# Local attention blocks: normalised keys to the block diagonal by DMA, and the low half of the first feed-forward weights on GpSimd

## The chip, the core and the metric

The kernel runs on one core of a Trainium2 chip. The metric is the device time of one execution in microseconds; the time before is the median of three runs. The engines are named as the profile names them: PE is TensorE (PEld its weight loads), DVE is VectorE, ACT is ScalarE, POOL is GpSimd, and SP is SyncE, which issues the DMAs of this kernel in one queue.

## The reference

The program runs eight layers on an activation of 4 to 8 sequences: a Mamba-like scan, a stack of local attention blocks, token attention, the same stack of local attention blocks again, linear attention, and three closing stages. The change touches only the two passes through the local attention stack. One stack has six levels, each of which is, cut to what matters:

```
for i in range(DEPTH):                       # 6 levels, 16 heads of 64, window 32
    x = attn_layer(shift_tokens(x), Wqkv[i], q_scale[i], k_scale[i], Wo[i]) + x
    x = ffn_layer(shift_tokens(x), ln_g[i], ln_b[i], W1[i], b1[i], W2[i], b2[i]) + x

attn_layer:  q, k = l2norm(q) * qs, l2norm(k) * ksc        # per token and head
             q, k = rotary(q) , rotary(k)
             softmax(mask(q @ [k of window before, k of own window].T * 8)) @ v
ffn_layer:   xn = layernorm(x) * g + bln
             a, gate = split(xn @ W1 + b1)                 # 341 + 341 columns
             a * gelu(gate) @ W2 + b2
```

Everything is float32.

## The kernel before

**Tiling.** The activation is 8 sequences of 256 tokens by 128 features, kept with features on the partitions and cut into NCH = 4 chunks of 512 tokens (two sequences). In the local stack the 16 heads are taken in 8 pairs. A *unit* is one chunk at one level, so a pass has 24 units of 8 pairs, and the loop in `steps` (L607) runs over the pairs of all units one after the other: 192 pairs in a pass, 384 in both, and some lead-in and run-out.

**Software pipeline.** One turn of that loop is a *step*. Each of its calls `do(what, ahead)` works on another pair: `rotate` on the pair 6 ahead, `prep` 1 ahead, `project` 7 ahead, `rounded` 5 ahead, `norms` and `norms_end` 6 ahead, `scores` on the current pair, `share` and `shared` 1 behind, `turn` and `attend` 2 behind. `feed` advances the feed-forward part of an older unit by one of 8 pieces a step. The loop stands under a manual schedule: each engine executes its instructions in the order in which this code writes them, and waits on semaphores for the others.

**Keys, lines 406 to 415.** `project` (L329) multiplies a pair's query and key weights with the chunk (three rounded float32 products, L213 to L215), copies both 128x512 results from PSUM to `raw` (ACT, L338), multiplies them with the cosine table into `tt` (DVE, L340), and has two DMAs swap the upper and lower 64 partitions of `raw` into `sw` (SP, L343 and L344). One step later `rotate` (POOL, L367 and L368) multiplies `sw` with the sine table and adds it to `tt`: `tt[:, 0]` is the rotated query and `tt[:, 1]` the rotated key. The squares go through ACT (L348) and PE (L359); every fourth pair the norms are finished on ACT and DVE (L131 to L146), four small DMAs (L388) bring them to 32 partitions, and ACT and POOL split them into a high and a low part (L397, L398). `prep` spreads the norms over a pair's 128 partitions by one matmul (PE, L410) into a PSUM bank `rb` and writes the normalised key into `kb`:

```
for h in range(2):
    nc.vector.scalar_tensor_tensor(kb[:, h, 32:], tt[:, 1], self.hcol[:, h:h + 1], rb, ALU.mult, ALU.mult)
```

`kb` is block-diagonal: 128 partitions, two column blocks, one for each head of the pair. `hcol[:, h]` holds one on the partitions of head h and zero elsewhere, so each of the two instructions writes a whole 128x512 block, half of it zeros. The 32-partition quarters 0 and 2 belong to head 0, and 1 and 3 to head 1. There are two `kb` buffers, zeroed once. `scores` (PE, L429) multiplies queries with `kb` one step later; DVE scales, masks, reduces and subtracts the scores (L437 to L440), ACT takes the exponential (L450), DVE the sums and reciprocals (L460, L461), POOL divides (L469), PE transposes (L482), ACT copies (L485), and PE multiplies with the values (L505).

**First feed-forward weights, lines 288 to 301.** `load_1` runs as a side generator that advances once a step. For each of the six column groups of `W1` (order 3, 4, 5, 0, 1, 2: the gate half first) it loads the raw weights in one step; in the next PE makes the bias (L296), ACT writes the high part scaled by the layer norm's gain (L298), DVE makes the low part in one instruction (L299), and DVE adds the bias (L301). It is queued at p = 7 of the last chunk's feed; the next unit's feed reads gate groups 3 to 5 at its p = 4 and groups 0 to 2 at its p = 6, one step a pair. `split` (L198) is the helper that other weights use: ACT writes the high part (L202) and POOL subtracts for the low part (L203), which is put into the list `top` and so issued first thing in the next step.

**PSUM.** Most products take their bank from a ring of six (`RING`), so a product waits until the bank's user of six takes ago has been read.

**Queue.** All DMAs here are issued by SP in program order. In the built program each DMA waits for the one that stands eight before it on SP, since eight semaphores are used in turn.

Of the kernel before, what the change touches and what calls it, by code (L numbers as in the profile page):

```python
# [11 lines left out]
F32R = mybir.dt.float32r  # L12
BF = mybir.dt.bfloat16
AF = mybir.ActivationFunctionType
ALU = mybir.AluOpType
# [6 lines left out]
NCH = 4  # L22
# [21 lines left out]
def f32(ap):  # L44
    return ap.bitcast(F32)


class Arena:
# [3 lines left out]
    def __init__(self, big, at=0, end=SIZE, rounded=None):  # L52
        self.big, self.at, self.end, self.tags, self.rounded = big, at, end, {}, rounded
# [164 lines left out]
class LocalBlock:  # L218


    def __init__(self, k):
        self.k, self.nkb = k, 0
        nc = k.nc
        R = Arena(k.bigr, 0, RSIZE)
        self.P = P = Arena(k.big, k.con.at, SIZE, R)
        self.D = k.D
        self.mask = k.const(P, "c_mask", (128, 512), BF)
        self.hcol = k.const(P, "c_hcol", (128, 2))
        self.sel = k.const(P, "c_sel", (128, 2, GP, 32))
        bsel = P.tile([128, GP, 128], F32, name="c_bsel", tag="rr", bufs=1)  # L230
        nc.sync.dma_start(out=bsel, in_=k.a["c_bsel"])
        self.bsel = P.tile([128, GP, 128], F32R, name="bsel")
        nc.vector.tensor_copy(self.bsel, bsel)
        self.qs = k.const(P, "qs", (128, DEPTH, 4))
        self.ffc = k.const(P, "lngb", (128, DEPTH, 2))
        self.b2 = k.const(P, "b2", (128, DEPTH))
        self.b1 = k.const(P, "b1", (128, DEPTH, 6))
        self.zero = P.tile([32, 128], BF, name="zero")
        self.kb = [P.tile([128, 2, 32 + CT], F32, name="kb_%d" % i) for i in range(NKB)]
        self.y = [P.tile([128, 2, 257], F32, name="y_%d" % c) for c in range(NCH)]  # L240
        for t in [self.zero] + self.kb + self.y:
            nc.vector.memset(t, 0.0)

        for tag, n, bufs in (("fx", 512, 2), ("sq", 512, 3), ("lny", 128, 2), ("nwt128", 128, 2),
                             ("tab0", 512, 2), ("tab1", 512, 2), ("wr_64", 512, NWR), ("wr_128", 256, NWR),
                             ("wvo", 512, NWV), ("bias1", 8, 2), ("w2", 128, 3)):
            P.place(tag, n, bufs)
        for tag, n, bufs in (("xs", 1024, 2), ("wqk", 512, 9), ("w1", 256, 7), ("fh", 1024, 1), ("rs", 512, 2)):
            R.place(tag, n, bufs)

        self.rs, self.nrs = [P.tile([128, CT], F32R, name="rs", tag="rs") for _ in range(2)], 0
        for t in self.rs:
            nc.vector.tensor_scalar(t, self.mask, 0.0, None, ALU.mult)
# [34 lines left out]
    def load_1(self, w, l):  # L288
        k, P, nc = self.k, self.P, self.k.nc
        w.bias1 = P.tile([128, 6], F32, name="bias1", tag="bias1", bufs=2)  # L290
        for i in (3, 4, 5, 0, 1, 2):
            m, o = (128, 128, 85)[i % 3], 341 * (i // 3) + 128 * (i % 3)
            r = self.raw(k.a["w1"][l, :, o:o + m], (128, m), "rw1")
            yield
            bp = k.bank(RING)
            nc.tensor.matmul(bp[:m, 0:1], r, self.ffc[:, l, 1:2], start=True, stop=True)  # L296
            hl = P.tile([128, 2, m], F32R, name="w1hl", tag="w1", bufs=7)
            nc.scalar.activation(hl[:, 0], r, AF.Copy, scale=self.ffc[:, l, 0:1])  # L298
            nc.vector.scalar_tensor_tensor(hl[:, 1], r, self.ffc[:, l, 0:1], f32(hl[:, 0]), ALU.mult, ALU.subtract)  # L299
            w.w1[i] = hl  # L300
            nc.vector.tensor_tensor(w.bias1[:m, i:i + 1], bp[:m, 0:1], self.b1[:m, l, i:i + 1], ALU.add)  # L301

    def load_2(self, w, l):
# [102 lines left out]
    def prep(self, u, p):  # L406

        k, nc, tt, rs = self.k, self.k.nc, u.t[p], u.rs[p // GP]
        rb = k.bank(RING)
        nc.tensor.matmul(rb, self.bsel[:, p % GP], rs, start=True, stop=True)  # L410
        kb = self.kb[self.nkb % NKB]
        self.nkb += 1
        for h in range(2):
            nc.vector.scalar_tensor_tensor(kb[:, h, 32:], tt[:, 1], self.hcol[:, h:h + 1], rb, ALU.mult, ALU.mult)  # L414
        u.kb[p] = kb

    def scores(self, u, p):
# [189 lines left out]
    def steps(self, us, ws, depth):  # L607
        NU, done, feed, side = len(us), [0] * NCH, None, []
        for i in range(-LEAD, 8 * NU + 20):
            def do(what, ahead):  # L610
                n, p = (i + ahead) // 8, (i + ahead) % 8
                if 0 <= n < NU:
                    what(us[n], p)
                    return us[n], p
                return None, p
            for f in self.top:
                f()
            self.top.clear()
            do(self.rotate, 6)
            do(self.prep, 1)  # L620
            do(self.share, -1)
            u, p = do(self.project, 7)
            do(self.rounded, 5)
            do(self.shared, -1)

            side = [g for g in side if next(g, side) is not side]
            if u:
                last = u.l + 1 == depth
                if u.c == NCH - 1 and not last:
                    side.append(self.load_qk(ws[u.l + 1], u.l + 1, p))  # L630
                    if p in (4, 5):
                        side.append(self.load_tab(ws[u.l + 1], u.l + 1, p - 4))
            do(self.norms, 6)
            do(self.norms_end, 6)
            n, p = (i - 12) // 8, (i - 12) % 8
            if 0 <= n < NU:
                u = us[n]
                last = u.l + 1 == depth
                if p == 0:
                    feed, fed = self.feed(u), u  # L640
                next(feed)
                if p == 7:
                    done[u.c] += 1
                    if u.c == NCH - 1 and not last:
                        side += [self.load_1(ws[u.l + 1], u.l + 1), self.load_2(ws[u.l + 1], u.l + 1)]
                    if last:
                        self.end(u.c)
            do(self.attended, -3)
            do(self.turn, -2)
            for f in self.mid:  # L650
                f()
            self.mid.clear()
            do(self.scores, 0)
            u, p = do(self.values, 2)
            if u and u.c == NCH - 1 and u.l + 1 < depth and p % 2 == 0:
                side.append(self.load_v(ws[u.l + 1], u.l + 1, p // 2))
            do(self.attend, -2)
            do(self.squares, 7)
            do(self.soft, 0)
            if feed and fed.late:  # L660
                self.k.nc.scalar.preload_act_table_set("natural_log_exp_and_others")
                fed.late = False
            n, p = (i + LEAD) // 8, (i + LEAD) % 8
            if p == 0 and 0 <= n < NU:
                u = us[n]
                assert done[u.c] == u.l
                u.xs = self.k.split(self.P, self.y[u.c][:, :, 0:256], (128, 2, 256), "xs", 2, self.top)
                u.xs = u.xs.rearrange("p h b t -> p h (b t)")
                if n + 1 < NCH:
                    side.append(self.begin(n + 1))  # L670
                    next(side[-1])
        assert not side
# [698 lines left out]
def constants():  # L1371
    f = np.float32
    h = np.arange(0, 64, 2, dtype=f)
# [9 lines left out]
    rot = np.zeros((128, 4, T), f)  # L1383
# [5 lines left out]
    i = np.arange(32)[:, None]  # L1389
    j = np.arange(64)[None]  # L1390
    m = np.zeros((128, 2, 4, 2, 32), f)
# [5 lines left out]
    sel = np.zeros((128, 2, GP, 32), f)  # L1397
    bsel = np.zeros((128, GP, 128), f)
    head = (np.arange(128) // 32) % 2
    for pl in range(GP):  # L1400
        for s_ in range(2):
            for h_ in range(2):
                row = 2 * GP * s_ + 2 * pl + h_
                sel[:, s_, pl, row] = head == h_
                if s_:
                    bsel[row:64:32, pl] = np.where(head == h_, f(-0.5), f(0))
    hcol = (head[:, None] == np.arange(2)[None]).astype(f)
    sm = (np.arange(128)[:, None] // 16 == np.arange(8)[None]).astype(f)
    d16 = np.arange(128) // 16
    dm = (d16[:, None] == d16[None]).astype(f)  # L1410
# [2 lines left out]
    p = np.arange(128)  # L1413
    sely = (2 * np.arange(16)[None, :, None] + p[:, None, None] // 64 == np.arange(32)[None, None]).astype(f)
    i2 = (p[:, None] % 64 == np.arange(64)[None]).astype(f)
    more = {"c_sely": sely, "c_i2": i2, "c_bmask": bm, "c_smask": sm, "c_dmask": dm, "c_hsel": hs}
    return {**more, "c_rot": rot, "c_mask": m.reshape(128, 512).astype("bfloat16"), "c_sel": sel, "c_bsel": bsel, "c_hcol": hcol}


def layout(i):  # L1420
# [55 lines left out]
def build(inputs, stages=None):  # L1476
    d = layout(inputs)
    d.update(constants())
    return {n: np.ascontiguousarray(v) for n, v in d.items()}
# [16 lines left out]
```

## Time and profile before

| what | value |
|---|---|
| median of 3 runs | 4397.36 us (4397.0 to 4401.22) |
| the profiled execution, its own time | 4402.16 us |
| its span, first to last instruction | 4400.4 us |
| first and last norm matmul of the local passes (L410) | 623.3 and 4006.4 us |
| norm matmuls (L410), one for each pair | 384 |
| L414 on DVE | 768 instructions, 537.7 us busy |
| granted PE clock, mean over the span | 0.922 |

The local passes lie between about 640 and 2190 us and between 2440 and 4010 us; what lies ahead, between and behind them is other code and is not touched. Within each pass PE stays at 9 tenths or more of every slice, and the page's clock row shows 9 tenths or more there. How to read the views: the busy share of an engine in a stretch says how full it is; the list of waits says which engine's instruction ended the idle time of another; the chain that ended last follows from the end of the program backwards what released what.

### The profile page before, as it was taken

How to read it: one execution, taken by the hardware profiler on the slowest of the kernel's cores; microseconds unless marked ns; L12 is line 12 of the kernel's file. 1: busy time of each engine (PE TensorE's matmuls, PEld its weight loads, DVE VectorE, ACT ScalarE, POOL GpSimd, SP SyncE). 2: the span in 40 equal slices, each digit the busy share in tenths (PEclk: the TensorE clock that was granted, in tenths of full speed). 3: DMA queues.
4: the chain of work that ended last, by engine and by line, in shares of the span. 5: the costliest groups of instructions: out<-in, count | busy, mean ns of one | idle time of the engine just before them, and what ended most of it. 6: DMA issues, size and time to landing. Idle time of an engine off the chain costs nothing.

```text
span 4400.4 us, 147972 instructions
## 1 busy us (share of the span) xinstructions
PE 3760.2 (85%) x64201; PEld 2852.7 (65%) x64201; DVE 3705.8 (84%) x5687; ACT 2645.0 (60%) x5050; POOL 3078.2 (70%) x1546
## 2 busy tenths in 40 slices
PE   5656679999999999999966899999999999997376
PEld 2222257777778778777744777787787777775144
DVE  6999958888888888888876788888888888887988
ACT  5423347767667677677544676676676767764322
POOL 3656668878778778787575887787877877862433
PEclk7777889999999999999966999999999999998578
DMA  0000033323233233333202332232333323221000
GB/s 19 7 3 16 1 78 81 89 74 89 72 75 90 73 85 74 78 82 76 54 20 68 81 90 72 69 93 72 88 74 74 87 71 92 72 71 42 15 6 10
DMA packets 134900, 272.97 MB, mean 62 GB/s; under 512 B 31020, under 2 KB 68328, under 8 KB 134248
## 3 DMA queue, kind: packets, MB, share of 16 engines
q1 hardware_dynamic: 134248, 263.51, 23.9%
q8 instruction: 503, 8.24, 0.8%
q14 instruction: 149, 1.22, 0.1%
HBM read 49.50 MB, written 6.29 MB: 13 GB/s over the span
## 4 chain that ended last, share of the span: by engine, by line
DVE 38%; PE 37%; ACT 13%; issue 8%; POOL 2%; DMA 2%; SPq 0%; DVEq 0%; POOLq 0%; ACTq 0%
PE pb L505 6%; PE pb L325 5%; DVE big L340 4%; DVE big L816 4%; DVE big L414 4%; PE pb L429 3%; DVE big L460 3%; PE pb L563 3%; PE pb L359 3%; DVE pb L438 2%; DVE big L439 2%; PE pb L410 2%; DVE pb L437 2%; DVE big L440 2%; ACT big L348 2%
## 5 line engine op out<-in xcount | busy, mean ns | idle before, releaser
L367 POOL TENSOR_TENSOR big<-big 128x1024 f32<-128x1024 f32 x384 | 916.0, 2385 | 405.0 <-DMA big<-big 319.7
L368 POOL TENSOR_TENSOR big<-big 128x1024 f32<-128x1024 f32 x384 | 917.2, 2389 | 30.1
L325 PE MATMUL pb<-big 128*32 128x128 f32 x24576 | 748.8, 274 | 4.3 <-DVE big L301 4.0
L414 DVE SCALAR_TENSOR_TENSOR big<-big,pb 128x512 f32<-128x512 f32 x768 | 537.7, 741 | 193.7 <-PE pb L410 153.3
L325 PEld LDWEIGHTS pb<-big 128*32 128x32 f32 x24576 | 681.6, 111 | 12.9 <-DVE big L301 7.1
L327 ACT COPY big<-pb 128x512 f32<-128x512 f32 x768 | 439.1, 597 | 317.8 <-PE pb L325 316.0
L338 ACT COPY big<-pb 128x512 f32<-128x512 f32 x768 | 440.1, 585 | 280.3 <-PE pb L215 248.6
L340 DVE TENSOR_TENSOR big<-pb,big 128x512 f32<-128x512 f32 x768 | 482.6, 668 | 43.6 <-ACT big L338 43.0
L469 POOL TENSOR_TENSOR big<-big 128x1024 f32<-128x1024 f32 x192 | 365.6, 1904 | 217.2 <-ACT big L348 133.6
L348 ACT ACTIVATE big<-big 128x512 f32<-128x512 f32 x768 | 443.4, 629 | 0.0
L505 PE MATMUL pb<-big 128*32 128x128 f32 x11520 | 402.0, 278 | 43.8 <-ACT big L485 35.0
L817 POOL TENSOR_TENSOR big<-big 128x1024 f32<-128x1024 f32 x128 | 305.3, 2398 | 191.4 <-DVE big L816 186.3
L213 PE MATMUL pb<-bigr 128*128 128x512 f32 (+1 forms) x1056 | 429.6, 407 | 11.3 <-ACT bigr L298 8.9
L215 PE MATMUL pb<-bigr 128*128 128x512 f32 (+1 forms) x1056 | 422.0, 400 | 4.2 <-DVE bigr L299 3.7
L429 PE MATMUL pb<-big 128*32 128x128 f32 x12288 | 418.6, 277 | 7.7 <-DVE big L440 4.7
L214 PE MATMUL pb<-bigr 128*128 128x512 f32 (+1 forms) x1056 | 420.1, 398 | 1.0 <-POOL bigr L203 1.0
L505 PEld LDWEIGHTS pb<-big 128*32 128x32 f32 x11520 | 325.3, 111 | 107.2 <-ACT big L485 91.4
L429 PEld LDWEIGHTS pb<-big 128*32 128x32 f32 x12288 | 314.9, 110 | 110.0 <-ACT big L338 32.7
L810 PE MATMUL pb<-bigr 128*128 128x512 f32 x512 | 214.0, 533 | 181.2 <-DVE big L816 124.6
L437 DVE TENSOR_TENSOR pb<-pb,big 128x512 f32<-128x512 f32 x384 | 266.4, 694 | 69.7 <-PE pb L429 67.3
L450 ACT ACTIVATE big<-big 128x1024 f32<-128x1024 f32 x192 | 203.7, 1061 | 191.5 <-DVE big L440 179.1
L359 PE MATMUL pb<-big 128*32 128x128 f32 x6144 | 296.4, 275 | 19.2 <-DVE big L146 8.6
(270 smaller groups left out, 7400.6 us busy)
## 6 DMA issues: line engine op xcount, KB each, us to landing
big<-big SPq DMA_DIRECT2D x768, 256.0 KB, 3.5
big<-in_wqk SPq DMA_DIRECT2D x96, 128.0 KB, 3.4
big<-x SPq DMA_DIRECT2D x28, 256.0 KB, 2.8
big<-in_c_rot SPq DMA_DIRECT2D x24, 256.0 KB, 4.9
big<-in_wv SPq DMA_DIRECT2D x48, 128.0 KB, 3.9
big<-in_wo SPq DMA_DIRECT2D x48, 128.0 KB, 3.3
big<-big SPq DMA_DIRECT2D x384, 16.0 KB, 2.4
x<-big SPq DMA_DIRECT2D x20, 256.0 KB, 3.9
```

Source lines behind the costliest of these rows:

```text
L213: mm(out, w[:, 0], x[:, 0], start=start, stop=False)
L325: nc.tensor.matmul(vp[32 * h:32 * h + 32, bass.ts(w, 128)], xw, wv[:, bass.ts(h, 128)], start=True, stop=True)
L327: nc.scalar.copy(v2[:, 4 * q:4 * q + 4].rearrange("p w f -> p (w f)"), vp)
L338: nc.scalar.copy(raw[:, s], ps)
L340: nc.vector.tensor_tensor(tt[:, s].rearrange("p (b t) -> p b t", b=2), ps.rearrange("p (b t) -> p b t", b=2), ct, ALU.mult)
L348: nc.scalar.activation(sq, raw[:, s], AF.Square)
L359: self.k.nc.tensor.matmul(u.nrm[32 * i:32 * i + 32, 0:128], self.sel[:, j, pl], q[:, bass.ts(i, 128)], start=(pl == 0 and j == 0), stop=(p ...
L367: nc.gpsimd.tensor_tensor(s4, s4, u.w.tab[1][:, :, None, :].broadcast_to([128, 2, 2, T]), ALU.mult)
L368: nc.gpsimd.tensor_tensor(tt, tt, sw, ALU.add)
L414: nc.vector.scalar_tensor_tensor(kb[:, h, 32:], tt[:, 1], self.hcol[:, h:h + 1], rb, ALU.mult, ALU.mult)
L429: mm(s4[32 * w:32 * w + 32, 2 * wg:2 * wg + 2], qf[:, 32 * win:32 * win + 32], kb[:, :, 32 * win:32 * win + 64].rearrange("p h (o j) -> p ...
L505: mm(u.acc[32 * w:32 * w + 32, bass.ts(wg, 128)], pts[o][:, 32 * win:32 * win + 32], v2[:, win - 1 + o], start=False, stop=(g == 3 and o = ...
```

## The change

`prep` multiplies the rotated key with the spread norms in place, with one DVE instruction, and four DMAs on SP copy the four 32-partition quarters to the diagonal blocks of `kb`. The off-diagonal blocks keep the zeros of the start, and the mask column `hcol` with its load is gone. `load_1` scales the raw weights in place on ACT and then uses the helper `split`: ACT writes the high part, POOL the low part in the next step. `load_1` is queued three steps earlier, at p = 4 of the last chunk's feed, behind that step's piece of `feed`; `load_2` stays at p = 7.

```
-        self.hcol = k.const(P, "c_hcol", (128, 2))
...
-            hl = P.tile([128, 2, m], F32R, name="w1hl", tag="w1", bufs=7)
-            nc.scalar.activation(hl[:, 0], r, AF.Copy, scale=self.ffc[:, l, 0:1])
-            nc.vector.scalar_tensor_tensor(hl[:, 1], r, self.ffc[:, l, 0:1], f32(hl[:, 0]), ALU.mult, ALU.subtract)
-            w.w1[i] = hl
+            nc.scalar.activation(r, r, AF.Copy, scale=self.ffc[:, l, 0:1])
+            w.w1[i] = k.split(P, r, (128, m), "w1", 7, self.top)
...
-        for h in range(2):
-            nc.vector.scalar_tensor_tensor(kb[:, h, 32:], tt[:, 1], self.hcol[:, h:h + 1], rb, ALU.mult, ALU.mult)
+        nc.vector.tensor_tensor(tt[:, 1], tt[:, 1], rb, ALU.mult)
+        for a in range(4):
+            rows = slice(32 * a, 32 * a + 32)
+            nc.sync.dma_start(out=kb[rows, a % 2, 32:], in_=tt[rows, 1])
...
+                if p == 4 and u.c == NCH - 1 and not last:
+                    side.append(self.load_1(ws[u.l + 1], u.l + 1))
                 if p == 7:
                     done[u.c] += 1
                     if u.c == NCH - 1 and not last:
-                        side += [self.load_1(ws[u.l + 1], u.l + 1), self.load_2(ws[u.l + 1], u.l + 1)]
+                        side.append(self.load_2(ws[u.l + 1], u.l + 1))
```

In the built program the order of all other instructions is the same on every engine. On DVE 768 L414 become 384, and 72 L299 go; ACT gains 72 instructions, POOL 72, and SP 1536 DMAs of 64 KB.

More of the change, by code (lines that the diff above doesn't have):

```diff
@@ L1406, in constants @@
                     bsel[row:64:32, pl] = np.where(head == h_, f(-0.5), f(0))
-    hcol = (head[:, None] == np.arange(2)[None]).astype(f)
     sm = (np.arange(128)[:, None] // 16 == np.arange(8)[None]).astype(f)
@@ L1416, in constants @@
     more = {"c_sely": sely, "c_i2": i2, "c_bmask": bm, "c_smask": sm, "c_dmask": dm, "c_hsel": hs}
-    return {**more, "c_rot": rot, "c_mask": m.reshape(128, 512).astype("bfloat16"), "c_sel": sel, "c_bsel": bsel, "c_hcol": hcol}
+    return {**more, "c_rot": rot, "c_mask": m.reshape(128, 512).astype("bfloat16"), "c_sel": sel, "c_bsel": bsel}
 def layout(i):
```

## The prediction

> **What bounds the kernel now.** I read the busy shares of the two local stretches first, since all that changes lies there, then who ends PE's waits, then the rows of the changed instructions and of the queues that get new work. In these windows the columns are microseconds, then PE, PEld, DVE, ACT and POOL busy, the granted clock, the DMA share and GB/s:
>
> ```profile
> 660.00:2180.00 1520.00, 1455.95 (x29513) 1181.52 (x29511) 1308.85 (x2085) 1063.28 (x2007) 1180.22 (x586) 1.00 0.32 79
> 2460.00:3980.00 1520.00, 1447.34 (x29224) 1176.11 (x29213) 1297.16 (x2062) 1058.29 (x1996) 1179.23 (x585) 0.99 0.32 78
> ```
>
> PE is busy 95.5%, DVE 86%, POOL 78%, ACT 70%. So PE sets the pace, at full clock, and a faster DVE can win only PE's idle time: 64.1 + 72.7 = 136.7 us. Who ends it (PE's waits in the first stretch; microseconds in total, times, longest):
>
> ```profile
> PE pb L505 <- ACT big L485: 16.3, 24, 1.4
> PE pb L563 <- DVE big L440: 13.5, 15, 1.1
> PE pb L482 <- DVE big L440: 5.1, 15, 1.5
> PE pb L482 <- POOL big L469: 4.6, 2, 3.2
> PE pb L213 <- ACT bigr L298: 4.4, 5, 0.9
> PE pb L296 <- DVE big L440: 4.1, 5, 0.9
> ...
> PE pb L215 <- DVE bigr L299: 1.9, 4, 0.5
> PE pb L410 <- POOL bigr L398: 1.8, 2, 1.5
> PE pb L325 <- DVE big L301: 1.6, 2, 0.8
> ```
>
> The reader is to see that DVE ends the most: all its rows of this list sum to 33.7 us, and to 42.6 in the second stretch; ACT's L298 adds 4.4 in each. That is 85 us of the 137. L440 is the last of a step's DVE work: PE needs a PSUM bank that DVE has not read yet, so DVE is late, by 0.9 us where it holds L563. Then the changed instructions and the queues:
>
> ```profile
> L414 DVE SCALAR_TENSOR_TENSOR big<-big,pb x768: 735/740/750, 623.8 to 4007.7; 128x512 f32<-128x512 f32 x192
> L299 DVE SCALAR_TENSOR_TENSOR bigr<-big,bigr x72: 299/1134/2424, 563.7 to 3908.9; 128x128 fp32r<-128x128 f32 x48, 128x85 fp32r<-128x85 f32 x24
> ...
> L343 SPq DMA_DIRECT2D big<-big x384: 461/462/513, 592.2 to 3961.9; - x192
> ...
> L388 SPq DMA_DIRECT2D big<-big x384: 507/589/1847, 613.6 to 3977.9; - x192
> ...
> DMA to landing us min/median/max: 1.8/2.4/4.4
> ```
>
> (ns, least, median, most; the last line is L388's, 16 KB each.) L414 is steady. L299, a quarter of its size, takes 299 ns at best and 2424 at worst: the one that started at 1519.03 us ended at 1521.2, just behind POOL's L368, which ran from 1518.7 to 1521.05. So it waits for POOL inside its own time.
>
> **The keys on DVE.** Two L414 of 741 ns go; one product of the same shape, from SBUF and PSUM to SBUF, comes. Its nearest row is L340, 668 ns. Per step 2 x 741 - 668 = 814 ns, over 384 steps 313 us of DVE. The loop's step is 8.2 us (1520 us hold 186), so DVE falls from 86% to about 76%. None of this is on the end's path by itself; it counts where PE waits for DVE.
>
> **The low part of W1.** L299's mean in the first stretch is 1.17 us (35.2 us for 30), so 60 in the loop are 70 us of DVE, in the steps in which DVE also makes PE wait at L296, L215 and L325. With POOL's L203 (732 ns at 128x256, so 0.37 to 0.73; I take 0.5) they become 36 us of POOL over all 72. ACT gains one copy each, L202, 394 ns at 128x256: 0.2 to 0.39, I take 0.35, 25 us. The three steps of lead matter as much: L213 waits for L298 once at each of the ten level changes, since the last group is made in the step that reads it. Started earlier, each group, POOL's next-step part included, is ready two steps or more before use, so L213 <- L298, L215 <- L299 and L325 <- L301 go (8.8 + 3.7 + 4.0 = 16.5 us). The raw buffer is now freed by POOL, at the head of the step after the high part; SP asks for it after that step's swaps, about when POOL reaches it.
>
> [...]
>
> **What PE gets back.** PE's rows give 85 us for DVE and L298. Matmul ends are modelled, and the same list for weight loads gives 72.3 + 79.2 for DVE and 13.2 for L298, 165 us; that is too much, as a weight load may wait while the matmul before it still runs. Between 85 and 165 I take 100, near PE's own rows. Not all goes: the 0.9 us waits at L563 and L296 are about what a step of DVE is relieved by, L482's 0.3 us waits lie well inside it, the W1 waits go, but single ones of 2 to 5 us at the edges of a pass only shrink. I take 80%: **-80 us**.
>
> **What is late next.** (a) The scores now need the four key DMAs. SP issues them at 0.46 + 3 x 0.59 = 2.2 us behind the product, and the last lands 2.4 us later (L388's row, 16 KB) to 3.8 (the 256 KB swap L344's median); 64 KB is nearest to the first. That is 4.7 to 6.1 us. From L414's start + 0.67 us to the L429 of the same pair the trace has 7.8 us at least in the full loop, and 5.6 in the run-out (2175.7 to 2181.3). So covered, by 1.7 us or more in the loop; without cover each microsecond costs 384. [...] The buffer is no new wait: PE executes the scores that free it before the L410 that starts this product.
>
> (b) Swaps queue behind the keys on SP. SP now waits for ACT's raw copies:
>
> ```profile
> SPq L343 <- ACT big L338: 952.8, 183, 10.8
> ...
> POOL big L367 <- DMA big<-big: 130.9, 66, 3.9
> ```
>
> That is 5.2 us of each step, which holds the 2.2 us of issues, but not where the product ends late. With the product's end as above, 0.06 us of wake-up and 2.2 us of issue against each swap's own issue time, the swaps leave 0.4 to 3.5 us later, 1.4 in the mean. The keys' 256 KB also move ahead of them: DMA is busy 0.32 of 8.2 us for some 640 KB, so at most 1.0 us. Each rotation on POOL then starts 1.4 to 2.4 us later where it waits for the swap (66 of 184 now). The rotated key has five steps of slack; but L469 and L398 stand behind the rotation on POOL. I moved every swap's landing by D, kept POOL's order and durations and all else, and counted where they end after the start of the PE instruction that reads them: at D = 1 us 0.5 us in all for L469 and 2.1 for L398, at 2 us 5 and 13, at 3 us 38 and 55, at 4 us 105 and 122. The two overlap in part. At D = 2 I take **+10**.
>
> (c) ACT's copy delays L485 in 60 steps, and about one step in four makes PE wait there (the two lists of both stretches have 180 such waits of weight loads and 48 of PE itself in 384 steps): 60 x 0.25 x 0.39 = **+6**; below nothing it cannot be. (d) PE, earlier, meets ACT's L485 more often: **+2**, bounds 0 and 35 (its present sum).
>
> Sum: -80 + 10 + 6 + 2 = **-62 us**. On the profiled execution's 4402.2 that is 4340; the median lies 4.8 lower, so 4397.4 - 62 = **4335 us**.
>
> **Rivals.**
> (1) *More goes* (chance 0.15): the weight-load rows are right, and most of 165 us goes: -100 to -150, about 4275. For it speaks that DVE is late by sums, so relief builds up from step to step; against it that PE has 137 us idle in all.
> (2) *The waits change hands* (0.11): PE is at 95.5%, and ACT's L485 (35 us), POOL and the DMAs take what DVE gives: -25 to +8, about 4390.
> (3) *Slower: the swap's delay reaches PE* (0.12). The mechanism is (b): four more DMAs ahead of two in one queue, rotation late, L469 and L398 behind it. From D = 3 us it costs 55 to 90 us and eats the gain; at D = 4 it costs about 140, so 4335 + 130 = 4465. For it: L469 of the sixth pair, which follows an L398, ends only 0.6 to 1.6 us before its reader in the middle half of the cases. Against it: D is 1.4 to 2.4 by the rows, and an earlier DVE lets the product end earlier, which shortens D.
> (4) *The keys don't get off the path* (0.03): landing takes 3 us more than the rows say, scores wait; 384 x 1 us and more, above 4700.
>
> **Numbers.** Forecast 0.59 at 4335, itself between 4300 and 4375. About 0.2% (9 us) is what a measurement here tells from no change. Faster by more: 0.59 + 0.15 + half of (2) = 0.79; within 0.2%: 0.06; slower: 0.15. The range takes in most of (1) and all of (2): 4275 to 4405 leaves out (3), (4) and the end of (1).
>
> **What would show it.** The product at about 670 ns, L440 gone from the waits of L563 and L296, and no wait of L213 for the high part of W1; DVE near 74% and PE above 97% in the local stretches; the keys' DMAs landing under 3.5 us and no DMA among L429's releasers; swaps landing 1.5 to 2.5 us later against ACT's copy, and rotation waiting for them in more steps. I am wrong if PE's waits for L469 and L398 grow past 30 us, if L429 waits for a DMA, or if ACT's L485 grows by what DVE loses.

## The result, and the profile after

| kernel | median us | lowest to highest | ratio to before |
|---|---|---|---|
| before | 4398.29 (4 runs) | 4397.0 to 4401.22 | 1 |
| after | 4446.43 (4 runs) | 4439.87 to 4449.64 | 1.0107, 95% interval 1.0089 to 1.0124 |

The changed kernel is 48 us **slower** where 62 us less were forecast. Its profiled execution took 4448.93 us (span 4447.2), and its mean granted PE clock is 0.913 where it was 0.922.

In the changed kernel the lines behind the removed mask column stand one to four lines earlier: the norm matmul L410 is now L407, the product on DVE L414 is L410, the key DMAs are L413, the swaps are L340 and L341 (before L343 and L344), the rotation L364 and L365, the norm split L395 (before L398), the division L468 (L469), the bias matmul of W1 L295 (L296), the scores L428 (L429), the last subtraction of a step on DVE L439 (L440), ACT's copy L484 (L485) and the product that reads it L504 (L505), and the wv by wo product of the weight load is L282 (L283), whose DMAs, like those of W1, are L257 (L258).

First the two local stretches of the changed kernel, with the columns of the prediction's table: microseconds, PE, PEld, DVE, ACT and POOL busy, granted clock, DMA share, GB/s.

```profile
660.00:2180.00 1520.00, 1444.62 (x29087) 1181.16 (x29083) 1140.53 (x1839) 1064.62 (x2016) 1182.62 (x612) 0.99 0.45 109
2460.00:3980.00 1520.00, 1442.09 (x28985) 1177.98 (x28977) 1141.33 (x1838) 1060.11 (x2013) 1182.43 (x612) 0.99 0.45 110
```

DVE has what it was to get: 75% busy where it was 86%. PE has not taken it up. It is busy 11 and 5 us less than before in the same 1520 us, and it executed 29,087 and 28,985 instructions there instead of 29,513 and 29,224. Something else has taken DVE's place in the list of PE's waits. The first stretch (the lists of waits take 640 to 2230 us as the first and 2440 to 4060 us as the second):

```profile
PE pb L282 <- DMA big<-in_wo: 19.4, 11, 3.2
PE pb L407 <- POOL bigr L395: 19.2, 17, 3.5
PE pb L295 <- DMA big<-in_w: 9.3, 9, 1.9
PE pb L562 <- DVE big L439: 9.3, 10, 1.1
...
PE pb L481 <- POOL big L468: 5.7, 4, 2.4
...
PE pb L504 <- ACT big L484: 1.9, 2, 1.2
...
PE pb L428 <- DMA big<-big: 0.3, 1, 0.3
```

Before, ACT's L485 headed this list with 16.3 us; its heir L504 <- L484 has 1.9. At the head now stand two kinds of row that hardly existed: PE waits for **DMAs of weights** (in_wo for L282, 1.3 us before; in_w for L295, 1.1 us before) and for **POOL's norm split** L395 (1.8 us before). With the second stretch they sum to 36.4, 20.9 and 40.1 us (3.8 of the last stand ahead of the second pass's first norm matmul), against 4.3, 2.5 and 2.5. The rows of before that were weight loads, first stretch:

```profile
PE pb L283 <- DMA big<-in_wo: 1.3, 2, 1.0
PE pb L296 <- DMA big<-in_w: 1.1, 2, 0.6
```

The scores (L428) wait for their key DMAs 0.3 us in all.

The changed instructions and the queue:

```profile
L410 DVE TENSOR_TENSOR big<-big,pb x384: 629/686/691, 626.9 to 4049.8; 128x512 f32<-128x512 f32 x192
L413 SPq DMA_DIRECT2D big<-big x1536: 507/588/2059, 627.6 to 4052.3; - x192
DMA to landing us min/median/max: 1.9/2.0/4.3
POOL big L364 <- DMA big<-big: 247.7, 98, 5.7
```

The product takes 0.69 us; the key DMAs, 0.59 us each in SP's queue, land in 2.0 us. The last row is the first stretch's wait of the rotation for its swap, 130.9 us in 66 waits before. I measured for each of the 384 steps the time from the end of ACT's second raw copy to the second swap: it is issued 0.64 us after the copy before and 2.47 us after it now (mean; a tenth of the steps 3.65 us or more), and, in the 46 and 53 steps where the trace tells the landing, it landed 4.59 and 6.38 us after it. The swaps are 1.8 us late.

The next lines tell what that does on POOL. They are the idle time of POOL just before the norm split, over the whole run (us, times), first in the kernel before (L398), then in the changed one (L395):

```profile
  ACT big L403: 108.2, 61
```

```profile
  ACT big L400: 13.6, 5
```

Before, POOL had reached its norm split early and waited there for its input, 108 us in 61 waits. That idle time was the slack; now 13.6 us of it are left, so the split starts when the rotation ahead of it on POOL is done, and the norm matmul L407 waits for it.

**One stall from near.** The granted clock in the changed kernel (same columns as above) around one wait for in_wo:

```profile
1610.00:1627.00 17.00, 16.69 (x352) 13.87 (x344) 13.38 (x21) 12.95 (x25) 16.69 (x12) 1.00 0.54 137
1627.00:1630.00 3.00, 0.20 (x1) 0.00 (x0) 2.12 (x4) 2.87 (x7) 2.93 (x2) 0.87 0.72 207
1630.00:1633.00 3.00, 2.96 (x10) 2.60 (x11) 0.00 (x0) 0.86 (x2) 2.99 (x2) 0.50 0.88 210
1633.00:1636.80 3.80, 3.80 (x32) 2.44 (x34) 0.00 (x0) 2.94 (x4) 3.80 (x3) 0.60 0.05 15
1636.80:1640.00 3.20, 3.20 (x99) 2.92 (x92) 2.62 (x4) 1.67 (x4) 2.82 (x2) 1.00 0.02 5
```

and its timeline (start, microseconds; in brackets the idle time before and its releaser), against the timeline of the same place in the kernel before, which follows it:

```profile
1625.35 0.50 SPq L257 DMA_DIRECT2D big<-in_wv  x1
1625.90 0.59 SPq L257 DMA_DIRECT2D big<-in_wo  x1
1626.62 2.45 SPq L413 DMA_DIRECT2D big<-big  x4
...
1630.05 2.04 PE L282 MATMUL pb<-big 64*128 64x128 f32 x8 [2.84 <-DMA big<-in_wo]
```

```profile
1607.90 0.60 SPq L258 DMA_DIRECT2D big<-in_wo  x1
...
1611.31 1.13 PE L283 MATMUL pb<-big 64*128 64x128 f32 x8 [0.25 <-DVE big L414]
```

The weights are loaded in one step and used in the next. Before, wo was issued 3.4 us ahead of its use, at 1607.90, and landed at 1611.17, 0.14 us before PE took it: no slack to speak of. In the changed kernel four key DMAs stand ahead of the loads in SP's queue and four more follow at once. PE stands idle for 2.84 us, and then the clock is at 0.50: the eight matmuls of L282 take 2.04 us where they took 1.13, and the project products that follow start every 0.43 us where they started every 0.23. In the last row, from 1636.8 us on, the clock is at 1.00 again. The step, from norm matmul to norm matmul, lasts 14.0 us here; at this place of the ten level changes it lasts 9.4 to 14.6 us, 8.4 to 9.7 before. The clock records of this trace have 1.00 and 0.50 and no other value; the 0.87 and 0.60 of the rows above are means. The clock fell from 1.00 to 0.50 at 1629.2 us, 2.0 us into an idle time of 2.84 us; it was at 1.00 again at 1636.1, 6.8 us later, of which PE worked 6.0.

### The profile page after: what moved, and what is told of

It is laid out like the page before. It is cut to its first block, busy times and chain, and to the rows that moved or that the text cites. A ratio compares the mean times of both kernels' runs of the same rounds, so it can differ in the third digit from the quotient of the medians.

```text
span 4447.2 us, 151030 instructions
## 1 busy us (share of the span) xinstructions
PE 3780.4 (85%) x64201; PEld 2878.9 (65%) x64201; DVE 3392.0 (76%) x5231; ACT 2670.6 (60%) x5122; POOL 3099.5 (70%) x1618
## 4 chain that ended last, share of the span: by engine, by line
PE 36%; DVE 28%; DMA 9%; ACT 8%; issue 8%; POOL 6%; SPq 5%; DVEq 0%; POOLq 0%; ACTq 0%
PE pb L322 5%; PE pb L428 4%; DVE big L817 4%; DMA big<-big 4%; PE pb L504 3%; PE pb L213 2%; SPq L413 2%; PE pb L214 2%; PE pb L215 2%; PE pb L562 2%; DMA big<-in_wo 2%; DVE pb L436 2%; DVE pb L437 2%; PE pb L481 2%; DVE big L438 2%
## 5 line engine op out<-in xcount | busy, mean ns | idle before, releaser
L364 POOL TENSOR_TENSOR big<-big 128x1024 f32<-128x1024 f32 x384 | 915.2, 2383 | 605.9 <-DMA big<-big 515.7
L365 POOL TENSOR_TENSOR big<-big 128x1024 f32<-128x1024 f32 x384 | 913.8, 2380 | 30.1
L322 PEld LDWEIGHTS pb<-big 128*32 128x32 f32 x24576 | 681.5, 110 | 10.2 <-DVE big L439 6.7
L337 DVE TENSOR_TENSOR big<-pb,big 128x512 f32<-128x512 f32 x768 | 492.1, 671 | 124.8 <-ACT big L335 120.7
L213 PE MATMUL pb<-bigr 128*128 128x512 f32 (+1 forms) x1056 | 436.9, 414 | 3.3 <-ACT bigr L202 1.5
L410 DVE TENSOR_TENSOR big<-big,pb 128x512 f32<-128x512 f32 x384 | 262.0, 682 | 220.0 <-PE pb L407 208.8
L214 PE MATMUL pb<-bigr 128*128 128x512 f32 (+1 forms) x1056 | 427.9, 405 | 1.0 <-POOL bigr L203 1.0
L215 PE MATMUL pb<-bigr 128*128 128x512 f32 (+1 forms) x1056 | 427.8, 405 | 0.0
L468 POOL TENSOR_TENSOR big<-big 128x1024 f32<-128x1024 f32 x192 | 365.5, 1904 | 88.1 <-DVE big L460 80.6
L428 PE MATMUL pb<-big 128*32 128x128 f32 x12288 | 424.0, 280 | 0.3 <-DMA big<-big 0.3
L504 PE MATMUL pb<-big 128*32 128x128 f32 x11520 | 394.4, 276 | 13.6 <-ACT big L484 7.4
L428 PEld LDWEIGHTS pb<-big 128*32 128x32 f32 x12288 | 318.9, 111 | 105.0 <-issue 37.6
L504 PEld LDWEIGHTS pb<-big 128*32 128x32 f32 x11520 | 324.8, 110 | 66.1 <-ACT big L484 52.2
L813 ACT ACTIVATE big<-pb,big 128x1020 f32<-128x1020 f32 x128 | 142.1, 1110 | 282.0 <-PE pb L811 191.7
```

The costliest lines, as they stand in the source:

```text
L213: mm(out, w[:, 0], x[:, 0], start=start, stop=False)
L214: mm(out, w[:, 0], x[:, 1], start=False, stop=False)
L215: mm(out, w[:, 1], x[:, 0], start=False, stop=stop)
L322: nc.tensor.matmul(vp[32 * h:32 * h + 32, bass.ts(w, 128)], xw, wv[:, bass.ts(h, 128)], start=True, stop=True)
L337: nc.vector.tensor_tensor(tt[:, s].rearrange("p (b t) -> p b t", b=2), ps.rearrange("p (b t) -> p b t", b=2), ct, ALU.mult)
L364: nc.gpsimd.tensor_tensor(s4, s4, u.w.tab[1][:, :, None, :].broadcast_to([128, 2, 2, T]), ALU.mult)
```

## The experiments

All medians stand against a kernel before of 4396.9 to 4399.0 us, measured beside each. The columns behind the ratio come from the profiled executions and cover the loops alone, from the first to the last norm matmul of each of the two passes: their length, PE's idle time by the kind of releaser (idle time for other reasons, at most 16 us, is left out), and the time at a granted clock of 0.50 (half clock), in pieces that begin in the loops.

| run | median us | ratio, 95% interval | loops us | PE idle: DVE / ACT / POOL / DMA us | half clock us |
|---|---|---|---|---|---|
| before | 4398.3 | 1 | 3144.1 | 77.4 / 45.6 / 5.5 / 7.0 | 30.7 |
| after | 4446.4 | 1.0107 (1.0089 to 1.0124) | 3184.1 | 51.5 / 9.4 / 44.0 / 57.4 | 102.4 |
| e1_keys_only | 4484.9 | 1.0196 (1.0181 to 1.0211) | 3224.8 | 63.8 / 35.9 / 39.4 / 63.0 | 88.7 |
| e2_w1_only | 4343.3 | 0.9877 (0.9860 to 0.9893) | 3083.7 | 61.7 / 17.5 / 5.5 / 5.0 | 13.7 |
| e3_one_dma | 4322.4 | 0.9825 (0.9811 to 0.9840) | 3058.5 | 50.6 / 3.3 / 9.4 / 9.3 | 23.9 |
| e4_four_small | 4427.8 | 1.0068 (1.0053 to 1.0083) | 3166.5 | 55.8 / 9.4 / 38.0 / 51.1 | 78.5 |
| e5_early_v | 4392.1 | 0.9988 (0.9979 to 0.9997) | 3131.1 | 51.5 / 14.9 / 44.2 / 17.5 | 61.4 |
| e6_keys_last | 4374.4 | 0.9944 (0.9929 to 0.9958) | 3115.2 | 47.7 / 14.8 / 7.2 / 44.9 | 27.3 |
| e7_keys_last_early | 4358.9 | 0.9907 (0.9890 to 0.9923) | 3105.1 | 50.0 / 15.1 / 8.8 / 41.2 | 20.5 |
| e8_move_only | 4393.8 | 0.9986 (0.9977 to 0.9995) | 3134.1 | 82.3 / 38.2 / 6.5 / 6.9 | 10.2 |
| e9_no_dma | 4298.7 | 0.9776 (0.9761 to 0.9790) | 3041.4 | 45.9 / 3.4 / 7.3 / 4.7 | 10.2 |
| e10_keys_act | 5043.5 | 1.1469 (1.1442 to 1.1497) | 3789.1 | 33.5 / 535.2 / 1.4 / 12.0 | 467.6 |
| e11_keep_busy | 4439.6 | 1.0101 (1.0082 to 1.0121) | 3176.8 | 49.8 / 15.5 / 40.9 / 31.8 | 44.4 |
| e12_w1_early | 4344.8 | 0.9880 (0.9866 to 0.9895) | 3086.5 | 59.5 / 20.4 / 5.4 / 4.2 | 13.7 |

### The two parts apart

**e1_keys_only**: the changed kernel with W1 as before.

```
-            nc.scalar.activation(r, r, AF.Copy, scale=self.ffc[:, l, 0:1])
-            w.w1[i] = k.split(P, r, (128, m), "w1", 7, self.top)
+            nc.scalar.activation(hl[:, 0], r, AF.Copy, scale=self.ffc[:, l, 0:1])
+            nc.vector.scalar_tensor_tensor(hl[:, 1], r, self.ffc[:, l, 0:1], f32(hl[:, 0]), ALU.mult, ALU.subtract)
...
-                if p == 4 and u.c == NCH - 1 and not last:
-                    side.append(self.load_1(ws[u.l + 1], u.l + 1))
```

> The keys by DMA as in the change; the W1 part is as before (low part on DVE, load_1 queued at p = 7). Theory Q (the queue: four more DMAs a step stand ahead of the swaps and of the next level's weight loads on SP, the loads reach PE late, and PE's clock falls to half after the longer waits): the loss is the keys' part, and the W1 part was a gain of some 20 us, so 4455 to 4475 us, with L282's and the last unit's growth as in the change. Rival W (the loss comes from the W1 part: its loads now wait for GpSimd and stand in other steps): about 4340 us, faster than before.

**e2_w1_only**: the kernel before with W1 as changed; DVE writes the keys with L414 twice, as before.

```
+                if p == 4 and u.c == NCH - 1 and not last:
+                    side.append(self.load_1(ws[u.l + 1], u.l + 1))
...
-            nc.vector.scalar_tensor_tensor(hl[:, 1], r, self.ffc[:, l, 0:1], f32(hl[:, 0]), ALU.mult, ALU.subtract)
+            nc.scalar.activation(r, r, AF.Copy, scale=self.ffc[:, l, 0:1])
+            w.w1[i] = k.split(P, r, (128, m), "w1", 7, self.top)
```

> The W1 part of the change alone; the keys are written by DVE as before. Theory Q: 4365 to 4385 us, since L213 <- L298, L215 <- L299 and L325 <- L301 go (16.5 us of PE's own idle rows) and DVE is relieved of 70 us. Rival W: 4440 us or more, with PE waiting for the W1 loads at L295.

The W1 part alone takes 53 us off, more than I expected of it; the keys part alone adds 88, some 10 us above my range. So the loss is the keys' alone. The two do not simply add: with the W1 part in place the keys part costs 103 us (4343.3 to 4446.4), 15 more than without it. The waits of PE in e2_w1_only, first stretch:

```profile
PE pb L503 <- ACT big L483: 9.6, 20, 0.8
...
PE pb L296 <- DVE big L438: 2.3, 5, 0.5
```

Both rows shrink (L503 is the L505 of before, 16.3 us; L296 had 4.1): the relief reaches PE through ACT's copy too. No row for the norm split or a weight DMA is among the first seven.

### The key DMAs: their number, their bytes, their absence

**e3_one_dma**: one DMA of the same 256 KB in place of four.

```
-        for a in range(4):
-            rows = slice(32 * a, 32 * a + 32)
-            nc.sync.dma_start(out=kb[rows, a % 2, 32:], in_=tt[rows, 1])
+        nc.sync.dma_start(out=kb[:, 0, 32:], in_=tt[:, 1])
```

> The change, but one DMA of 128 partitions x 512 (256 KB) in place of the four of 64 KB: the same bytes with one issue. It writes head 1's keys into head 0's block, so the scores are not the reference's; the work is otherwise the same. Theory Q: the issue time on SP falls from 2.4 to 0.6 us a step, PE's waits for the wv/wo and W1 loads fall from 57 to under 20 us, the units of the last chunk from 75 to 69 us: 4350 to 4385 us. Rival B (bytes: 96 MB more through the DMA engines make every landing later): unchanged, 4435 to 4455 us.

**e4_four_small**: four DMAs, each of 32 columns, 4 KB.

```
-            nc.sync.dma_start(out=kb[rows, a % 2, 32:], in_=tt[rows, 1])
+            nc.sync.dma_start(out=kb[rows, a % 2, 32:64], in_=tt[rows, 1, 0:32])
```

> The change, but each of the four key DMAs moves only the first 32 of 512 columns (4 KB): the same issues with a sixteenth of the bytes. Most keys are left out, so the scores are not the reference's. Theory Q: unchanged or slightly less, 4425 to 4450 us, since the issues stand in the queue as before. Rival B: 4340 to 4370 us.

**e9_no_dma**: the changed kernel without the key DMAs.

```
-        for a in range(4):
-            rows = slice(32 * a, 32 * a + 32)
-            nc.sync.dma_start(out=kb[rows, a % 2, 32:], in_=tt[rows, 1])
```

> The change without its key DMAs: DVE makes the product, nothing brings it to the score blocks, which stay zero (keys left out of the scores, so the output is not the reference's). With the W1 part alone as its base (4343 us) it measures what DVE's relief of 0.8 us a step is worth when nothing is paid for it. Theory M (the term of the keys was mis-sized: PE sets the pace and little of DVE's 313 us was ever on its path): 4310 to 4325 us, 20 to 35 less than the W1 part alone, near the run with one DMA (4322). Rival F (the forecast's size was right and the one DMA already took part of it back): 4285 to 4300 us.

Without the DMAs the time is 4299, with the four it is 4446: **the four DMAs cost 148 us**. One DMA with all their bytes costs 24; four with a sixteenth of the bytes cost 129. So the bytes cost little here (19 us), and the number of issues much: SP spends 0.48 to 0.59 us at the median on each, whether it moves 4, 64 or 256 KB. The issues of e4_four_small (4 KB, L413) and of e3_one_dma (256 KB, L411):

```profile
L413 SPq DMA_DIRECT2D big<-big x1536: 507/589/1864, 624.9 to 4032.5; - x192
L411 SPq DMA_DIRECT2D big<-big x384: 466/478/586, 625.2 to 3921.5; - x192
```

With one DMA the second swap leaves 0.80 us after ACT's copy, with the four small ones 2.44 us, so it is not the wait for the product either, which stands ahead of the swaps in both. A further rival lies in the program: each DMA waits for the one that stands eight before it, and four more in a step bring that one nearer. SP's own waits speak against it: inside the loops it waited 7 times, 18 us in all, for the landing of a DMA, and 7 times, 21 us, in the kernel before.

e3_one_dma came out some 28 us below my range; e9_no_dma came out at the upper end of what it was to show if the forecast's size without the DMAs was right. The first stretch of e3_one_dma, with the columns of the stretches above:

```profile
660.00:2180.00 1520.00, 1476.20 (x29926) 1206.85 (x29924) 1177.64 (x1900) 1081.86 (x2056) 1197.69 (x620) 0.99 0.40 111
```

PE is busy 97.1% with all the keys' traffic on the DMA engines (111 GB/s, 109 in the changed kernel): it is not the traffic that held PE up. e3_one_dma writes one block where two are wanted, so it is no way out. It shows that one issue in place of four was worth 124 us (4446.4 against 4322.4).

### The order in SP's queue

**e5_early_v**: the changed kernel with the wv and wo loads issued at the end of the step that queues them, ahead of the next step's keys and swaps instead of behind them; PE uses them where it did.

```
     def load_v(...):
         yield
+        if self.top is not None:
+            yield
...
                     side.append(self.load_v(...))
+                    next(side[-1])
```

> The change, with the wv and wo loads of the next level issued half a step to a step earlier: at the end of the step that queues them instead of behind the next step's keys and swaps; PE uses them in the same step as before. Theory Q: PE's wait for in_wo (36 us) goes, and with it the stretches of half clock behind it, so the units of the last chunk fall from 74 us to about 69: 4380 to 4410 us; the waits for L395 (40 us) and in_w (21 us) stay. Rival S (the swaps' delay on GpSimd, that is L395 and L468, carries the loss and the loads only wait beside it): 4430 us or more.

**e6_keys_last**: the changed kernel with the four key DMAs of a step behind its swaps and weight loads, as a method of their own.

```
+    def place(self, u, p):
+        kb, tt = u.kb[p], u.t[p]
+        for a in range(4):
+            rows = slice(32 * a, 32 * a + 32)
+            self.k.nc.sync.dma_start(out=kb[rows, a % 2, 32:], in_=tt[rows, 1])
...
+            do(self.place, 1)
             do(self.norms, 6)
```

> The change, with the four key DMAs moved behind the step's swaps and weight loads in SP's order; the product on DVE stays where it is. Theory Q: the swaps and loads leave as early as before the change, so PE's waits for L395, in_wo and in_w fall to what they were (3, 4 and 3 us), the half clock goes, and DVE's relief is left: 4315 to 4345 us. Rival K (the scores then wait for the keys, which have only about one microsecond to spare): L428 waits for DMAs in most steps, 4400 us or more. Rival B (bytes): 4430 us or more.

**e7_keys_last_early**: both edits.

> Keys behind the swaps and loads as in the run before, and the wv and wo loads issued early as in the first. Theory Q: nothing is left to win for the loads, so the same as the run before within 8 us; if the keys behind them were late in the steps with five loads, 5 to 15 us faster than it. Rival S: the same as the run before.

**e12_w1_early**: e2_w1_only (no key DMAs) with the early loads of e5_early_v.

> The W1 part alone with the wv and wo loads issued early; keys by DVE as before. A candidate for the best version. Theory Q: there PE waits only 5 us in all for DMAs and 5 of that for in_wo at most, so 4335 to 4345 us, the same as or just under the W1 part alone (4343).

The early loads give back 54 us where key DMAs stand in the queue, and nothing where none do (e12_w1_early against e2_w1_only: 4344.8 and 4343.3). That separates the price of a late weight load from any good of loading early as such. In e5_early_v the rows of in_wo are gone from the head of the list, and POOL's row stays, with 18.3 us in the first stretch (L409 and L397 are its norm matmul and split):

```profile
PE pb L409 <- POOL bigr L397: 18.3, 19, 3.2
```

Moving the keys behind swaps and loads (e6_keys_last) gives back 72. The swaps are then issued 0.74 us after ACT's copy (0.64 before), POOL's idle time ahead of its norm split is back at 104.4 us, and PE's idle time by POOL falls from 44.0 to 7.2 us. This undoes the delay of the swaps and of the loads and leaves the rest of the change, and e5_early_v, which undoes that of wv and wo alone, leaves POOL's row; so the path swap, rotation, norm split, norm matmul is shown. I had expected at least 30 us more of it; the bill comes elsewhere. PE's waits of e6_keys_last, first stretch (L432 is its scores line):

```profile
PE pb L432 <- DMA big<-big: 17.0, 17, 1.9
...
PE pb L407 <- POOL bigr L395: 4.3, 7, 0.9
```

The scores now wait for the keys, 17.0 us here and 20.1 in the second stretch. With both edits the time is 4358.9, still 15.6 us above e2_w1_only, where DVE writes the keys: with four DMAs the keys by DMA did not pay in either place of the queue that I tried.

**e10_keys_act**: the late place of e6_keys_last, the four DMAs issued by ACT instead of SP.

```
-            self.k.nc.sync.dma_start(out=kb[rows, a % 2, 32:], in_=tt[rows, 1])
+            self.k.nc.scalar.dma_start(out=kb[rows, a % 2, 32:], in_=tt[rows, 1])
```

> Keys' DMAs at the late place (behind the swaps and loads in program order), but issued by ACT's queue in place of SP's. Theory Q (what costs is the place in SP's one queue): PE's waits for loads, swaps and keys all go, and what is paid is ACT's issue time; at the 0.5 to 0.6 us that SP needs for one that is 2.2 us of a step in which ACT is free for 2.5, so ACT is near full: 4340 to 4420 us, with SP's row as free as before and L484 and L284 late behind ACT. Rival D (four small DMAs a step cost by themselves, whoever issues them): 4370 to 4390, as with SP at that place, with L428 waiting for DMAs.

It costs 669 us against e6_keys_last. The DMAs of e10_keys_act (L418), and PE's greatest wait in its first stretch:

```profile
L418 ACTq DMA_DIRECT2D big<-big x1536: 513/654/2434, 629.2 to 4657.4; - x192
```

```profile
PE pb L508 <- ACT big L488: 190.3, 61, 4.5
```

Four issues of 0.65 us are 2.6 us in a step in which ACT was already busy 70% of 8.2 us, that is 5.7: together 8.3. My expectation had this sum, at SP's price of 2.2 us, and called ACT near full. What it left out is that ACT executes the DMAs and the waits before them in its own order: ahead of L131, which works on the norms and reads no key, ACT sat idle 23 times until one of L418's DMAs had landed, 69.9 us in all. A step of e10_keys_act lasts 9.9 us (3789.1 us for 384), well over 8.3, so more than the issues' own time is paid; how the rest divides was not measured.

### The parts of W1, and the clock

**e8_move_only**: the kernel before with `load_1` queued at p = 4, all else as before, the low part on DVE.

```
+                if p == 4 and u.c == NCH - 1 and not last:
+                    side.append(self.load_1(ws[u.l + 1], u.l + 1))
```

> The kernel before, with load_1 alone queued three steps earlier (p = 4); DVE still makes the low part, the keys are written by DVE. It splits the 53 us that the W1 part alone gained. Theory L (the lead is what counts: L213 no longer waits for a group made in the same step): 4355 to 4375 us, and the low part on GpSimd is worth the other 15 to 25. Rival P (the low part on GpSimd is what counts, as DVE no longer waits for GpSimd within L299 in steps where PE waits for DVE): 4380 to 4395 us.

The three steps of lead bring 4.5 us, as rival P had it. The waits of L213 and L215 for W1 go, all 12.6 us of them. But PE waits for DVE at the bias in their place; the two stretches' rows of L296 <- L440 sum to 26.1 us where they had 8.6. The first stretch of e8_move_only:

```profile
PE pb L505 <- ACT big L485: 18.5, 26, 1.4
PE pb L296 <- DVE big L440: 12.9, 14, 1.7
```

So the other 49 us of the W1 part are the low part's leaving DVE: e2_w1_only against e8_move_only, 4343.3 and 4393.8. In e2_w1_only L296 has 2.3 us, and ACT's row half of what it has here.

**e11_keep_busy**: the changed kernel with five extra products, which nothing reads, ahead of the first wv by wo product of each level.

```
         wp = k.bank(RING)
+        if self.top is not None and g == 0:
+            for _ in range(5):
+                nc.tensor.matmul(wp, k.cmat, k.one.rearrange("p s j -> p (s j)"), start=True, stop=True)
```

> The change, with five extra 128x512 float32 products (0.43 us each, constants, into the bank that the real ones overwrite) ahead of the first wv/wo product of each level, so that PE works while it would wait some 2 us there. Theory H (half of that stall's price is the halved clock behind the idle time): the wait is no shorter but the clock stays up, so the ten level changes lose 2 to 3 us less each: 4415 to 4430 us, and the stretches of half clock of the last chunk's units go. Rival N (the clock falls for another reason, or costs nothing on the path): 4446 us or up to 20 more, as the extra products take PE's time where there was no wait.

The time at half clock falls from 102 to 44 us and the idle time for DMAs by 26, but the median only by 7, within what the intervals overlap. The products are not free: PE is busy with them for 44.5 us, twice what I had counted, since each of the 50 is two matmul records 0.43 us apart. So this run does not size the clock's share. The table goes further, but not to the end. PE's time in the loops that is *not* idle (length less all idle time) is 2979.2 us in e9_no_dma. In the five kernels with the most half clock it is longer by 42.5 us (after), 43.4 (e1), 33.0 (e4), 23.7 (e5) and 227.8 (e10), for 92.2, 78.5, 68.3, 51.2 and 457.4 us more at half clock: 0.46 to 0.55 us for each. That fits work that takes twice as long in that time. But the kernels in which DVE writes the keys are longer too, by 27.2 us (before), 14.5 (e2), 19.6 (e8) and 16.2 (e12), with only 20, 3, 0 and 3 us more at half clock, so something else moves this time as well. It is an association, not an edit that changes the clock alone, and the clock's share is not shown.

## Why the prediction was wrong

**The step that failed is (b) of "What is late next"**, "Swaps queue behind the keys on SP", taken at +10, with nothing for the weight loads that stand behind the same keys. The four key DMAs cost about 148; without them the sum was 28 us too cautious.

1. *What PE gets back*, -80, with +6 and +2 behind it: -72 were to be the change without queue effects. e9_no_dma, which is that, is 100 us below the kernel before, measured beside it. The mechanism was right, the size too small by 28, at the edge of rival 1's -100 to -150.
   - The W1 part measured -53. I had put its lead forward ("the three steps of lead matter as much", 16.5 us of rows), and those rows do go, but the lead brought 4.5 us because the waits changed hands to L296 (rival 2's mechanism, inside e8_move_only). What brought 49 is the 70 us of DVE time, in the steps where DVE was late anyway. Moved to POOL, the instructions cost PE nothing that shows: its idle time by POOL in the loops is 5.5 us before and in e2_w1_only. For 128x128 POOL takes 0.46 us in the mean (L203 in the changed kernel) where DVE took 0.98 (L299 before).
   - The keys' DVE relief measured -45 (4298.7 against 4343.3).
   - (c) and (d), +8, had the wrong sign: ACT's L485 was to get worse, and its rows fell from 34.6 us in both stretches to 7.0. With less on DVE, ACT is in time. Nor did L440 leave the waits of L563: 13.5 us became 9.3 in the first stretch, and it is 10.3 without any key DMA.
2. *(a) The scores wait for the keys*: covered, as said. 2.0 us of landing, 0.3 us of waiting in all. The cover ends in e6_keys_last, 37 us in both stretches.
3. *(b) The swaps*: the delay itself was right, 1.8 us in the mean within the forecast 1.4 to 2.4. Two things were wrong.
   - Its price. I took the mean D, and 13 and 5 us at 2 us by a model that kept every other time of the kernel before. Inside the loops PE paid 36.2 us at the norm split and 7.8 at the division, 2.5 and 3.0 before. A tenth of the steps had a delay of 3 us and more, where the same model had 55 and 38 us; and the faster kernel has less slack by itself (POOL's idle time before the split is 57.7 us in e9_no_dma, 108.2 before). How these two share is not shown. The prediction's sign of failure, PE's waits for L469 and L398 past 30 us, is what the profile has: rival 3, chance 0.12, is part of what happened.
   - What else is behind the keys. I followed the queue to the swaps and stopped. The same queue carries the **weight loads** of the next level, wv and wo for L283 and W1 for L296, used one step after their issue. Their slack was in the list of waits that I had read (in_wo 1.3 and 3.0 us, in_w 1.1 and 1.4: already the last to arrive), and no term and no rival priced them. They came to 57.3 us of idle PE; loading wv and wo early, whose rows are 36.4 of these, gave 54 back, 34 of it idle time in the loops and 19 PE time that is not idle, with 41 us less at half clock.
4. *The clock.* No term priced what a PE stall costs beyond its length. The loops of the changed kernel are 142.6 us longer than those of e9_no_dma: 100.1 idle and 42.5 in which PE worked longer at the same instructions, with 92 us more at half clock; how much of the 42.5 is the clock's stays open, as said.
5. *The sum.* -53 (W1) - 45 (keys off DVE) + 148 (four DMAs) = +50; measured +48.1 us. The sum takes the parts in this order; in another the W1 part is worth 38.5 us (4484.9 against 4446.4, both with the keys by DMA).

Steps of "What would show it" that held: the product at 0.69 us, no wait of L213 for the high part, DVE near 75%, keys landing under 3.5 us at the median (the longest took 4.3), swaps about 2 us later, the rotation waiting more often (98 waits, 66 before). PE above 97% held in the first stretch of e3_one_dma and e9_no_dma and not in the changed kernel.

The kernel to keep is e2_w1_only: W1 as changed, the keys as before, 4343.3 us, 1.2% below the kernel before (interval 1.1% to 1.4%).

## What to carry to other kernels

An instruction that costs its engine 0.7 us and hides for the most part can be dearer to remove than to keep, if what replaces it goes into an in-order queue: list *every* transfer behind the new ones in that queue, with its consumer and the slack it has, not the nearest alone, and count issues before bytes (here four DMAs of 4 KB a step cost 129 us, and 64 KB instead of 4 another 19). Rows of one microsecond in the list of waits tell where slack is already zero; whatever delays such a row is paid at once (in_wo, 1.3 us before, 19.4 after), and on PE a slower clock can come on top (0.50 for 6.8 us at the stall of 2.84 us). Where a relief and a delay come in one change, the relief can also eat the slack that the delay was to hide in: the keys part cost 88 us alone and 103 on top of the W1 part.

## What the runs showed of the hardware that I had not expected

- A DMA of 4, 64 or 256 KB takes SP about the same issue time, 0.59, 0.59 and 0.48 us at the median for the keys, and four of 4 KB cost nearly what four of 64 KB do: 129 us against 148.
- An idle time of 2.84 us within a stretch in which PE is 95% busy was enough for the granted clock to fall to 0.50, 2.0 us after its start, and it stayed there for 6.8 us. In the loops of the changed kernel there were 22 such pieces, 102 us in all, against 8 and 31 us before.
- DMAs issued by a busy ACT take 0.65 us each of ACT's own order; 1536 of them, with the waits that they brought into it, made the kernel 669 us longer than the same DMAs issued by SP.
- The same subtraction of 128x128 that DVE does in 0.3 to 2.4 us, and costs PE some 49 us in the loops, costs PE nothing that shows on POOL, which is 78% busy. In the trace of the kernel before, 52 of the 72 on DVE (48 of 128x128, 24 of 128x85) took 0.66 us or more, and each of these ended 0.10 to 0.16 us after an instruction of POOL that had run beside it; the other 20 took 0.30 to 0.40. So the long ones ended just behind POOL's, as the prediction read it from one of them; no run here took POOL's reads away to test what holds it.
